# A DiT block: q and k by feature through VectorE's 32x32 transposes and DRAM instead of TensorE's transposes

## The chip, the cores and the metric

The kernel runs on one core of one Trainium2 chip, in one launch, in float32. A core has TensorE (PE, with the weight loads shown apart as PEld), VectorE (DVE), ScalarE (ACT), GpSimd (POOL) and SyncE (SP). SP, ACT and POOL also issue DMAs; in the profile the queue of SP is SPq. The metric is the device time of the launch in microseconds (us), the median of the runs; smaller is better.

## The reference

The input x is [2, 2048, 576]: batch 2, 2048 tokens, 576 features; 16 heads of 36 features; the hidden layer of the MLP has 2304. The condition c gives six rows of 576 by one product (shift, scale and gate for the attention part and for the MLP).

```python
mod = silu(c) @ w_ada + b_ada          # sh_msa, sc_msa, g_msa, sh_mlp, sc_mlp, g_mlp
xn  = ln(x, 1e-6) * (1 + sc_msa) + sh_msa
qkv = (xn @ w_qkv + b_qkv).reshape(B, N, 3, 16, 36)
q   = ln(q, 1e-5, qn_g, qn_b)          # over the 36 features of a head
k   = ln(k, 1e-5, kn_g, kn_b)
attn = softmax(einsum('bqhd,bkhd->bhqk', q, k) * 36 ** -0.5)
o   = einsum('bhqk,bkhd->bqhd', attn, v).reshape(B, N, 576) @ w_proj + b_proj
x   = x + g_msa * o
xn2 = ln(x, 1e-6) * (1 + sc_mlp) + sh_mlp
x   = x + g_mlp * (gelu(xn2 @ w1 + b1) @ w2 + b2)
```

The gain and bias of the head norms (qn_g, qn_b, kn_g, kn_b) have one value for each of the 36 features of a head. They are what the change calls scale and bias.

## The kernel before

`block_of_small` is the path that runs with these inputs. For each of the two batches it has three stages, and after both the MLP follows (two products with 7 instead of 8 sub-products each, at 2184 to 3176 us).

**Inputs** (`inputs`, about 62 to 251 us in the first batch, 1110 to 1329 in the second). A loop over the 16 token tiles of 128 tokens. In each turn TensorE makes three products, q, k and v (`product`: two halves of 288 columns, four matmuls on whole chunks and two on the last one each); VectorE adds the bias as it takes them out of PSUM (`biased`); `centred` subtracts each head's mean; ScalarE squares the result into `sq`; `head_scale` of the tile before takes the variance, ScalarE its root, VectorE the reciprocal, and GpSimd multiplies (`both` times `inv`). `by_feature(t - 2, ...)` then turns the finished q and k rows of the tile two back into columns: nine TensorE transposes of 128x128 into PSUM (line 993), and nine evictions, each applying gain and bias per partition: c < 4 by ScalarE (line 998), the other five by VectorE (line 1002). The result lies in SBUF, features on partitions: chunks 0 to 4 in `qo`, 5 to 8 in `kr`. Beside it runs the preparation of the rows two tiles on: the load of x, its norm on VectorE, a 32x32 transpose of all blocks on VectorE (`squares_turned`, line 898), four DMAs from GpSimd's queue that put the squares in their transposed places in a DRAM tensor `turned` (line 903), and DMAs that read it back by feature (`xnt`), which ScalarE modulates.

**Attention** (`attend`, about 251 to 1032 us and 1329 to 2104). 128 steps over (pair of heads, block of 512 queries, group g of keys). In each step TensorE makes `scores` (8 key-by-query banks: 32 features of a head in `km`, `qm`, the other 4 split into a high and a low part in `ke`, `qe`), ScalarE takes the exponential of 8 banks, and TensorE makes `values` of the step before. `take_q`, `take_k` and `take_k_block` issue the DMAs that bring the rows of a pair of heads into `qm`, `qe`, `km`, `ke` (`rows_taken`), and return a function (`parted`: two VectorE operations per 512 columns) that is called later. In the inputs they are started by `by_feature` itself: after tile 3 the first q block and key tiles 0 to 3, after tiles 7, 11, 13 and 15 the key tiles up to there; the returned function is called in the next `by_feature`, before the next tile is turned over. The last two tiles are turned by the `hooks` of the first steps of attention: nine transposes each, in two parts, at steps (0,0,0), (0,0,1), (0,1,0) and (0,1,1).

**Outputs** (`outputs`): the projection, its gate and the residual, and in the first batch the preparation of the second's inputs. Unused parts of `kr` serve as row buffers (`spare`).

The order on TensorE and VectorE is that of the program (`manual_schedule`), in attention also that of GpSimd and ScalarE; the order on the DMA queue of SP, and on ScalarE and GpSimd in the inputs, is set by a scheduler. Each queue runs its instructions in order: an instruction that waits holds up all behind it. In the inputs PSUM is four tiles of two banks (`s_tile`), each taken by one product, or by half of the transposes of a tile; in attention eight single banks.

Of the kernel before, what the change touches and what calls it, by code (L numbers as in the profile page):

```python
# [31 lines left out]
def dit_block(  # L32
# [230 lines left out]
    gb_qk = const.tile([P, 2, NQK], F32, name="gb_qk")  # L263
    gain_qk, bias_qk = gb_qk[:, 0, :], gb_qk[:, 1, :]
# [23 lines left out]
    with psum_pools(), tc.tile_pool(name="ada", bufs=2) as ada:  # L288
        raw = ada.tile([P, NKC, B], F32, name="raw")
        nc.sync.dma_start(out=raw[:, 0:FULL, :], in_=cond_t[0:512, :].rearrange("(p k) b -> p k b", k=FULL))  # L290
        for r0 in (0, 64):
            nc.sync.dma_start(out=raw[r0 : r0 + 64, FULL, :], in_=cond_t[512:576, :])
        nc.sync.dma_start(out=x_first[:, :C], in_=x[0, 0:P, :])
        was = ada_weights(ada, (1, 0))
        nc.gpsimd.memset(sil, 0.0)
        nc.scalar.activation(sil[:, :, 0:B], raw, AF.Silu)
        first_biases = feature_biases(ada, (1, 0), nc.gpsimd)
        rows_dram = dram.tile([2, 2, H, HD], F32, name="rows_dram")
        gb_rows = ada.tile([2 * NQK, P], F32, name="gb_rows")
        for i, ins in enumerate(((qn_g, kn_g), (qn_b, kn_b))):  # L300
            for w in range(2):
                nc.gpsimd.dma_start(out=rows_dram[i, w], in_=ins[w].partition_broadcast(H))
        nc.gpsimd.dma_start(
            out=gb_rows, in_=rows_dram.rearrange("i w h d -> (i w h d)").rearrange("(c p) -> c p", p=P)
        )
        rows_normed(ada, x_first)

        turned = s_tile()
        for k in range(NKC):
            nc.tensor.transpose(  # L310
                turned[:, k // FULL, k % FULL * P : (k % FULL + 1) * P], x_first[:, k * P : (k + 1) * P], ident
            )
        nc.scalar.copy(x_first[:, :512], turned[:, 0, :])
        nc.scalar.copy(x_first[:, 512:], turned[:, 1, :P])
        features(feature_rows(ada, was, first_biases), (1, 0))
        gb_ps = s_tile()[:, 0, : 2 * NQK]
        nc.tensor.transpose(gb_ps, gb_rows, ident[: 2 * NQK, : 2 * NQK])
        nc.vector.tensor_copy(gb_qk.rearrange("p i c -> p (i c)"), gb_ps)
# [440 lines left out]
    def block_of_small():  # L759
# [25 lines left out]
        high = kv.tile([P, BLK], F32R, name="high")  # L785
        met = kv.tile([1, 1], F32, name="met")
# [16 lines left out]
        def chunk(c, cols):  # L803
            return qo[:, c, cols] if c < NKC else kr[:, c - NKC, cols]


        def rows_taken(queue, main, ends, halves, first, src, dst):

            for c in halves:
                for h in range(2):  # L810
                    r0 = 32 * (2 * c + h)
                    for i, row, d, n in head_rows(first + h * HD, DIMS):
                        queue.dma_start(out=main[r0 + d : r0 + d + n, dst], in_=chunk(i, src(c))[row : row + n, :])
                    ((i, row, _, n),) = head_rows(first + h * HD + DIMS, HD - DIMS)
                    values = chunk(i, src(c))[row : row + n, :]
                    queue.dma_start(
                        out=ends[r0 : r0 + 4 * n, dst],
                        in_=values.unsqueeze(1).to_broadcast([n, 4, values.shape[1]]),
                    )

        def parted(ends, rows, low, sign):

            n = min(ends.shape[1], BLK)
            for c0 in range(0, ends.shape[1], n):
                part, up = ends[rows, c0 : c0 + n], high[rows, :n]
                nc.vector.tensor_scalar(up, part, sign[rows, :], None, ALU.mult)
                nc.vector.scalar_tensor_tensor(
                    part.bitcast(F32R), part, low[rows, :], up.bitcast(F32), ALU.mult, ALU.add
                )

        def take_k(p):
            m, e = km[p % 2], ke[p % 2]
            if p > 2:
                not_sooner(m)
                not_sooner(e)
            src = lambda c: slice(c * N // 2, (c + 1) * N // 2)
            rows_taken(nc.gpsimd, m, e, range(2), C + p * 2 * HD, src, slice(0, N // 2))
            return lambda: parted(e, slice(0, P), low_k, sign_k)

        def take_k_block(t0, t1):  # L840

            c, k0 = divmod(t0 * P, N // 2)
            dst = slice(k0, k0 + (t1 - t0) * P)
            rows_taken(nc.sync, km[0], ke[0], (c,), C, lambda c: slice(t0 * P, t1 * P), dst)
            return lambda: parted(ke[0][:, dst], slice(64 * c, 64 * c + 64), low_k, sign_k)

        def take_q(p, qb):
            i = qb % 2
            src = lambda c: slice(qb * BLK, (qb + 1) * BLK)
            rows_taken(nc.sync, qm[i], qe[i], range(2), p * 2 * HD, src, slice(0, BLK))  # L850
            return lambda: parted(qe[i], slice(0, P), low_q, sign_q)
# [94 lines left out]
        def inputs(b, weights, work, xnt, rows, loaded):  # L946
# [5 lines left out]
            def banks_of_two():  # L952
                return [bank for ps in (s_tile(), s_tile()) for bank in (ps[:, 0], ps[:, 1])]

            def centred(both, w0=0, w1=2):
# [10 lines left out]
                if w0 == 0:  # L966
                    squares["sq"] = work.tile([P, 2 * C], F32, name="sq")
# [20 lines left out]
            def by_feature(t, banks, chunks=range(NQK), all_on_vector=False, per=4):  # L988
                both, begun = normed[t], [*taken]
                taken.clear()  # L990
                parts = [(c, banks[i // per][:, i % per * P : i % per * P + P]) for i, c in enumerate(chunks)]
                for c, ps in parts:
                    nc.tensor.transpose(ps, both[:, c * P : (c + 1) * P], ident)  # L993

                for c, ps in parts[::-1]:
                    dst = chunk(c, slice(t * P, (t + 1) * P))
                    if c < 4 and not all_on_vector:
                        nc.scalar.activation(
                            dst, ps, AF.Identity, bias=bias_qk[:, c : c + 1], scale=gain_qk[:, c : c + 1]
                        )  # L1000
                    else:
                        nc.vector.tensor_scalar(
                            dst, ps, gain_qk[:, c : c + 1], bias_qk[:, c : c + 1], ALU.mult, ALU.add
                        )
                for do in begun:
                    do()
                if t == TPB - 1:
                    taken.append(take_q(0, 0))
                if t + 1 in key_tiles and NQK - 1 in chunks:
                    i = key_tiles.index(t + 1)  # L1010
                    taken.append(take_k_block(*key_tiles[i - 1 : i + 1]))

            def last(t, chunks):


                per = 3 if b == 0 and len(chunks) > 4 else 4
                by_feature(t, [bank() for _ in range(0, len(chunks), per)], chunks, True, per)
                left = [*taken]
                taken.clear()
                return left  # L1020
# [33 lines left out]
            for t in range(NT - 2):  # L1054
# [20 lines left out]
                biased(2, v, t, both)  # L1075
                if t >= 2:
                    by_feature(t - 2, banks_of_two())
# [4 lines left out]
            for t in range(NT - 2, NT):  # L1082
# [3 lines left out]
                for w in range(3):  # L1086
# [5 lines left out]
                    if w == (1 if t % 2 == 0 else 0):  # L1092
                        if t + 1 < NT:
                            input_modulated(b, ahead)
                        by_feature(t - 2, banks_of_two())
# [7 lines left out]
                before, xnt = both, ahead  # L1103

# [4 lines left out]
        def attend(b, pool, hooks):  # L1109
# [64 lines left out]
            behind, later = None, [[] for _ in range(5)]  # L1174
            for p, qb, g in [*steps, (None, None, None)]:
                pts = None if p is None else scores(p, qb, g)
                if g == 0 and (p, qb) != (NPAIR - 1, NBLK - 1):
                    later[2].append(take_q(*((p, qb + 1) if qb + 1 < NBLK else (p + 1, 0))))
                if g == 1 and qb == 1 and p + 1 < NPAIR:
                    later[4].append(take_k(p + 1))  # L1180
# [28 lines left out]
        spare = [kr[:, c, a * 640 : a * 640 + C] for c in range(4) for a in range(3)]  # L1209
# [115 lines left out]
        for b in range(B):  # L1325
# [11 lines left out]
            def last_inputs_done():  # L1337
                last_inputs(NT - 1, range(NKC - 1))
                close_work()

# [17 lines left out]
            def output_opened():  # L1358
# [3 lines left out]
                (0, 0, 0): lambda: last_inputs(NT - 2, range(NKC - 1, NQK)),  # L1362
                (0, 0, 1): lambda: last_inputs(NT - 1, range(NKC - 1, NQK)),
                (0, 1, 0): lambda: last_inputs(NT - 2, range(NKC - 1)),
                (0, 1, 1): last_inputs_done,
# [35 lines left out]
            if b + 1 < B:  # L1401
# [5 lines left out]
                def turned_of(t):  # L1407
                    squares = spare[9 + t % 3]
                    return (lambda x1: first.append(squares_turned(x1, nc.gpsimd, squares))) if t <= TPB else None

                with tc.manual_schedule(engines={mybir.EngineType.DVE}):
                    outputs(b, wp, {12: [lambda: input_modulated(b + 1, xnt)]}, spare[:9], turned_of)
# [389 lines left out]
```

## Time and profile before

| | |
|---|---|
| median of 3 runs | 3178.82 us (3177.3 to 3179.14) |
| profiled execution, its own time | 3178.22 us |
| its span in the profile | 3176.4 us |
| TensorE busy in the span | 3152.3 us, 99% |
| VectorE, ScalarE, GpSimd busy | 48%, 48%, 21% |
| granted TensorE clock, mean | 0.999 |

The span is what the profiler saw; the own time of that execution is 1.8 us more and lies 0.6 us under the median. Busy is the time in which an engine had an instruction in work; overlapping matmuls count once. "Released by" or "<-" names what ended a wait.

### The profile page before, as it was taken

Reading aid. Unit: us, or ns where it says so; the run is one execution under the profiler, and the core shown is the slowest. Engines: PE = TensorE matmul, PEld = TensorE weight load, DVE = VectorE, ACT = ScalarE, POOL = GpSimd, SP = SyncE. Lnnn points to the kernel's source line nnn. Section 1 sums busy time; section 2 is a strip of 40 time slices with the busy share of each in tenths; the row PEclk is TensorE's granted clock in tenths of the full one; section 3 lists DMA queues with packets and bytes.
Section 4 is the critical chain, followed back from the end, with each engine's and each line's share of the span. In section 5 each row is a group of like instructions: output and inputs, shape, how many; then the busy total and the mean of one; then the engine's idle time right before and its main releaser. Section 6 shows DMA issues by size and latency. Waiting matters only on the chain.

```text
span 3176.4 us, 47350 instructions
## 1 busy us (share of the span) xinstructions
PE 3152.3 (99%) x17833; PEld 1892.8 (60%) x17833; DVE 1511.0 (48%) x2212; ACT 1515.4 (48%) x2953; POOL 670.3 (21%) x933
## 2 busy tenths in 40 slices
PE   8999999999999999999999999999999999999999
PEld 6884333333333788733333333358888888777777
DVE  5774333333333577633333333346566554445454
ACT  2335666666666034466666666643555552000000
POOL 4551000112110355400001111013333320212121
PEclk9999999999999999999999999999999999999999
DMA  5322212223221633211222223146544434333331
GB/s 150 77 66 69 74 34 69 65 71 80 66 75 41 196 69 73 61 53 44 50 46 65 69 64 72 51 154 206 159 136 137 133 109 154 118 124 112 119 105 39
DMA packets 154537, 290.04 MB, mean 91 GB/s; under 512 B 34419, under 2 KB 86844, under 8 KB 152188
## 3 DMA queue, kind: packets, MB, share of 16 engines
q1 hardware_dynamic: 106212, 170.47, 17.7%
q0 software_dynamic: 44544, 110.85, 14.0%
q10 hardware_dynamic: 3544, 5.60, 0.5%
q8 instruction: 143, 2.34, 0.3%
q14 instruction: 94, 0.77, 0.1%
HBM read 153.95 MB, written 84.63 MB: 75 GB/s over the span
## 4 chain that ended last, share of the span: by engine, by line
PE 98%; DVE 1%; DMA 1%; SPq 0%; ACT 0%; issue 0%; ACTq 0%; DVEq 0%
PE b L1140 29%; PE b L1127 19%; PE s L1714 15%; PE m L1555 12%; PE s L1033 11%; PE s L413 4%; PE m L1569 2%; PE one L1555 2%; PE s L1035 1%; PE s L993 1%; PE s L424 1%; DMA bq<-in_w_qkv_dram 0%; DMA wq<-in_w_qkv_dram 0%; PE b L192 0%; DVE var L973 0%; DMA km<-qo 0%
## 5 line engine op out<-in xcount | busy, mean ns | idle before, releaser
L1131 ACT ACTIVATE pt<-b 128x512 f32<-128x512 f32 x2048 | 1057.8, 608 | 486.3 <-PE b L1140 272.2
L1140 PE MATMUL b<-pt,vt 128*64 128x512 f32 x4096 | 935.0, 598 | 0.0
L1140 PEld LDWEIGHTS b<-pt,vt 128*64 128x64 f32 x4096 | 271.8, 136 | 582.0 <-issue 439.4
L1127 PE MATMUL b<-qm,km 32*128 32x512 f32 x4096 | 568.1, 614 | 0.9 <-DVE vt L1044 0.6
L1188 DVE TENSOR_TENSOR ot<-b,ot 128x512 f32<-128x512 f32 x192 | 132.8, 692 | 652.2 <-PE b L1140 651.7
L1127 PE MATMUL b<-qe,ke 16*128 16x512 f32 x2048 | 423.7, 790 | 0.0
L1033 PE MATMUL s<-wq,xnt 128*128 128x288 f32 x1536 | 406.6, 408 | 3.6 <-DMA wq<-in_w_qkv_dram 2.8
L1127 PEld LDWEIGHTS b<-qm,km 32*128 32x128 f32 x4096 | 192.3, 184 | 270.5 <-ACT pt L1131 208.4
L1714 PE MATMUL s<-ws,as 128*128 128x288 f32 x1440 | 351.8, 406 | 0.0
L1033 PEld LDWEIGHTS s<-wq,xnt 128*128 128x128 f32 x1536 | 281.7, 191 | 65.8 <-DVE rstd L278 3.0
L1714 PEld LDWEIGHTS s<-ws,as 128*128 128x128 f32 x1440 | 273.6, 190 | 75.6
L1159 DVE RECIPROCAL den<-den 128x512 f32<-128x512 f32 x64 | 213.6, 3337 | 9.3 <-DMA den<-den_dram 9.3
L1555 PE MATMUL m<-xnt,wb 128*128 128x256 f32 x864 | 210.2, 379 | 0.9 <-issue 0.9
L1555 PE MATMUL m<-s,wb 128*128 128x256 f32 x864 | 210.0, 379 | 0.0
L1186 DVE COPY ot<-b 128x512 f32<-128x512 f32 x64 | 44.3, 692 | 334.0 <-PE b L1140 334.0
L903 POOL DMA_DIRECT2D turned<-squares x220 | 148.3, 680 | 258.7 <-DVE squares L898 235.3
L1555 PEld LDWEIGHTS m<-s,wb 128*128 128x128 f32 x864 | 164.2, 190 | 22.3
L1127 PEld LDWEIGHTS b<-qe,ke 16*128 16x128 f32 x2048 | 108.3, 184 | 114.4 <-issue 113.1
L1555 PEld LDWEIGHTS m<-xnt,wb 128*128 128x128 f32 x864 | 158.9, 190 | 20.3 <-issue 1.3
L1244 POOL DMA_DIRECT2D kr<-in_x_dram x32 | 17.6, 549 | 726.9 <-DVE met L790 726.9
L1593 ACT ACTIVATE cs<-cs,b_sb 128x512 f32<-128x512 f32 x144 | 98.8, 719 | 115.1 <-DVE cs L1588 93.1
L1714 PE MATMUL s<-ws,hidden 128*128 128x288 f32 x576 | 142.3, 406 | 0.0
(199 smaller groups left out, 3012.0 us busy)
## 6 DMA issues: line engine op xcount, KB each, us to landing
gelu<-cs SPq DMA_DIRECT2D x144, 256.0 KB
hidden<-gelu SPq DMA_DIRECT2D x16, 2304.0 KB
den<-den_dram SPq DMA_DIRECT2D x128, 128.0 KB
turned<-squares POOLq DMA_DIRECT2D x220, 72.0 KB, 2.5
xnt<-turned POOLq DMA_DIRECT2D x56, 256.0 KB, 3.8
x_dram<-kr POOLq DMA_DIRECT2D x48, 288.0 KB, 3.4
qm<-qo SPq DMA_DIRECT2D x192, 64.0 KB
kr<-in_x_dram POOLq DMA_DIRECT2D x34, 288.0 KB, 3.8
```

The source lines that it names most:

```text
L413: nc.tensor.matmul(outs[a], stationary(k, a), moving(k, a), start=(first and k == 0), stop=(not first and k == FULL - 1),)
L903: queue.dma_start(out=by_square[g], in_=squares[g * SQ : (g + 1) * SQ, :].rearrange("p (k j) -> p k j", j=SQ))
L1033: nc.tensor.matmul(out_a, full[:, k, :], wq[:, k, f], start=k == 0, stop=False)
L1127: nc.tensor.matmul(ps, k[r, keys], q[r, :], start=first, stop=not first)
L1131: nc.scalar.activation(pt[:, h, :], banks[2 * c + h], AF.Exp, scale=SCALE)
L1140: nc.tensor.matmul(acc[64 * h : 64 * h + 64, :], vt[:, v0 : v0 + 64], pt[:, h, :], start=pt is pts[0][0], stop=pt is pts[-1][0],)
L1159: nc.vector.reciprocal(den, den)
L1188: nc.vector.tensor_tensor(ot, acc, ot, ALU.add)
L1555: nc.tensor.matmul(out_m[m], wb[:, slot[m], k, f * P : (f + 1) * P], moving[m](k), start=k == 0 and m in (1, 2, 5, 6), stop=k == 1 and m == 1,
L1569: nc.tensor.matmul(out_m[m], wr[w][:, f * P : (f + 1) * P], a[:, i, t * PAIR : (t + 1) * PAIR], start=False, stop=i == 1 and m != 2,)
L1593: nc.scalar.activation(part, part, AF.Gelu, bias=b1_sb[:, g : g + 1])
L1714: nc.tensor.matmul(ms[m], stationary[m][:, f, :], ws[m][:, f, :], start=(f == 0), stop=(f == HF - 1))
```

## The change

`by_feature` no longer uses TensorE and PSUM. VectorE transposes all 32x32 blocks of the tile's q and k rows at once (128x1152) into one of three parts of `kr`, and four DMAs on SP's queue write them into a DRAM tensor `qk` of [1152, 2048], features by tokens, in runs of 32 values. `rows_taken` reads its rows from there, so one DMA serves the 32 features where one or two stood before. Gain and bias are applied in attention to the rows taken: `scaled` on `qm` and `km`, and inside `parted` on `qe` and `ke`, with the values by row from `gb_at`, which two small matmuls with a selection make once (`gains_by_row`, after tile 1 of the first batch). The buffer `sq` moves into `kr`. The last two tiles are turned over at the end of the inputs and in the first step of attention, not in four steps of it. `spare` has 11 buffers and `outputs` of the first batch uses 8 row buffers instead of 9.

```diff
-        gb_rows = ada.tile([2 * NQK, P], F32, name="gb_rows")
+        nc.gpsimd.memset(gb_rows, 0.0)
...
-                nc.gpsimd.dma_start(out=rows_dram[i, w], in_=ins[w].partition_broadcast(H))
+                nc.gpsimd.dma_start(out=gb_rows[:HD, i, w : w + 1], in_=ins[w].unsqueeze(1))
...
-        nc.tensor.transpose(gb_ps, gb_rows, ident[: 2 * NQK, : 2 * NQK])
-        nc.vector.tensor_copy(gb_qk.rearrange("p i c -> p (i c)"), gb_ps)
...
         def rows_taken(queue, main, ends, halves, first, src, dst):
-                    for i, row, d, n in head_rows(first + h * HD, DIMS):
-                        queue.dma_start(out=main[r0 + d : r0 + d + n, dst], in_=chunk(i, src(c))[row : row + n, :])
+                    queue.dma_start(out=main[r0 : r0 + DIMS, dst], in_=qk_rows["dram"][f0 : f0 + DIMS, src(c)])
...
+        def gains_by_row():
+            at = {i: kr[:, i, 2 * C : 2 * C + P] for i in range(2)}
...
+            nc.vector.tensor_copy(
+                at[0][0:DIMS, :].rearrange("p (i d) -> p i d", d=DIMS),
+                ident[0:DIMS, 0:DIMS].unsqueeze(1).to_broadcast([DIMS, 4, DIMS]),
+            )
+            for i in range(4):
+                nc.vector.tensor_copy(
+                    at[1][DIMS : 2 * DIMS, 32 * i : 32 * i + 16].rearrange("p (d r) -> p d r", r=4),
+                    ident[DIMS : 2 * DIMS, DIMS:HD].unsqueeze(2).to_broadcast([DIMS, 4, 4]),
+                )
+            ps = s_tile()[:, 0, 0:8]
+            for i, sel in at.items():
+                nc.tensor.matmul(
+                    ps[:, 4 * i : 4 * i + 4], sel, gb_rows.rearrange("p i w -> p (i w)"), start=True, stop=True
+                )
+            nc.vector.tensor_copy(gb_at.rearrange("p e i w -> p (e i w)"), ps)
+
+        def scaled(dst, part, rows, w, of_ends=0):
+            gain, bias = (gb_at[rows, of_ends, i, w : w + 1] for i in range(2))
+            nc.vector.tensor_scalar(dst, part, gain, bias, ALU.mult, ALU.add)
 
-        def parted(ends, rows, low, sign):
+        def parted(ends, rows, w):
...
-                nc.vector.tensor_scalar(up, part, sign[rows, :], None, ALU.mult)
+                scaled(value, part, rows, w, 1)
+                nc.vector.tensor_scalar(up, value, sign[rows, :], None, ALU.mult)
...
         def take_k_block(t0, t1):
...
-            return lambda: parted(ke[0][:, dst], slice(64 * c, 64 * c + 64), low_k, sign_k)
+            def made():
+                scaled(km[0][rows, dst], km[0][rows, dst], rows, 1)
+                parted(ke[0][:, dst], rows, 1)
+            return made
...
         def take_q(p, qb):
-            return lambda: parted(qe[i], slice(0, P), low_q, sign_q)
+            return [lambda: scaled(qm[i], qm[i], full, 0), lambda: parted(qe[i], full, 0)]
...
-            def by_feature(t, banks, chunks=range(NQK), all_on_vector=False, per=4):
-                for c, ps in parts:
-                    nc.tensor.transpose(ps, both[:, c * P : (c + 1) * P], ident)
-                for c, ps in parts[::-1]:
...
+            qk_rows["dram"] = dram.tile([2 * C, N], F32, name=f"qk{b}")
+            by_square = qk_rows["dram"].rearrange("(k d) (t g j) -> t g d k j", d=SQ, g=P // SQ, j=SQ)
+            def by_feature(t):
+                squares = kr[:, t % 3, 0 : 2 * C]
+                nc.vector.transpose(squares, normed[t])
+                for g in range(P // SQ):
+                    nc.sync.dma_start(
+                        out=by_square[t, g], in_=squares[g * SQ : (g + 1) * SQ, :].rearrange("p (k j) -> p k j", j=SQ)
+                    )
                 for do in begun:
                     do()
...
+                if b == 0 and t == 1:
+                    gains_by_row()
                 if t >= 2:
-                    by_feature(t - 2, banks_of_two())
+                    by_feature(t - 2)
...
+            by_feature(NT - 2)
...
-                    later[2].append(take_q(*((p, qb + 1) if qb + 1 < NBLK else (p + 1, 0))))
+                    for i, do in enumerate(take_q(*((p, qb + 1) if qb + 1 < NBLK else (p + 1, 0)))):
+                        later[1 + i].append(do)
...
-                (0, 0, 0): lambda: last_inputs(NT - 2, range(NKC - 1, NQK)),
-                (0, 0, 1): lambda: last_inputs(NT - 1, range(NKC - 1, NQK)),
-                (0, 1, 0): lambda: last_inputs(NT - 2, range(NKC - 1)),
-                (0, 1, 1): last_inputs_done,
+                (0, 0, 0): last_inputs_done,
```

## The prediction

> **What bounds the kernel now.** I read the page's busy times and its chain first, then TensorE's timeline in the inputs and at the opening of attention, then busy time and DMA share by stretch, then the groups that the change touches.
>
> ```profile
> PE 3152.3 (99%) x17833; PEld 1892.8 (60%) x17833; DVE 1511.0 (48%) x2212; ACT 1515.4 (48%) x2953; POOL 670.3 (21%) x933
> ...
> PE 98%; DVE 1%; DMA 1%; SPq 0%; ACT 0%; issue 0%; ACTq 0%; DVEq 0%
> ```
>
> TensorE runs without a gap and the chain lies on it, so what leaves its queue shortens the kernel unless a wait takes its place. How long the nine transposes of a tile hold the queue is read from starts, not from durations that overlap:
>
> ```profile
> 80.09 1.15 PE L993 MATMUL s<-ident,both 128*128 128x128 f32 x9
> 81.08 2.11 PE L1033 MATMUL s<-wq,xnt 128*128 128x288 f32 x8
> ...
> 94.30 1.15 PE L993 MATMUL s<-ident,both 128*128 128x128 f32 x9
> 95.28 2.11 PE L1033 MATMUL s<-wq,xnt 128*128 128x288 f32 x8
> ```
>
> They take 0.98 us of a tile's 14.21; the products are 13.22. What stands beside it in such a tile and over the inputs (columns: span, then PE, PEld, DVE, ACT, POOL busy, clock, DMA share, GB/s):
>
> ```profile
> 80.09:94.30 14.21, 14.21 (x72) 11.69 (x71) 10.84 (x19) 5.59 (x13) 8.79 (x11) 1.00 0.35 76
> ...
> 62.00:250.00 188.00, 188.00 (x918) 154.79 (x917) 145.33 (x257) 72.38 (x167) 95.64 (x122) 1.00 0.29 66
> ```
>
> VectorE is busy 77% of the inputs, the DMA engines 29%, about 4 us of a tile. The groups:
>
> ```profile
> L993 PE MATMUL s<-ident,both 128*128 128x128 f32 x252 | 32.1, 272 | 0.0
> L1002 DVE TENSOR_SCALAR kr<-s,gb_qk 128x128 f32<-128x128 f32 x112 | 38.1, 402 | 5.8 <-PE s L993 5.8
> L898 DVE STREAM_TRANSPOSE squares<-xt 128x576 f32<-128x576 f32 x37 | 28.8, 779 | 1.3
> L826 DVE TENSOR_SCALAR high<-qe,part 128x512 fp32r<-128x512 f32 x64 | 30.6, 478 | 0.1
> L827 DVE SCALAR_TENSOR_TENSOR qe<-qe,part,high 128x512 fp32r<-128x512 f32 x64 | 48.1, 751 | 2.3
> ```
>
> **Removed.** 14 groups of nine in each batch's input loop: 28 x 0.98 = 27.4 us. The other two tiles of a batch are turned in attention (0.7 + 0.7 + 0.6 + 0.6 us); these I count with the opening below. ScalarE loses four evictions a tile, VectorE five; neither is on the path.
>
> **Moved to VectorE, in the inputs.** Five evictions (starts to end about 2.0 us) give way to one transpose of 128x1152: twice the 779 ns less the fixed part, 1.5 us. VectorE's tile, waits on ScalarE included, adds up to 11.5 us of 13.2: covered, with 1.7 us to spare; without that cover each us over costs 28 us. Here the Trainium skill ("VectorE: DVE Perf Modes", "Rules for kernel authors") speaks against the change: transpose 128x128 on TensorE if PSUM will do. Its table in "The three transpose paths" has 390 ns on TensorE and 311 on VectorE, 32x32 blocks only. The trace has 0.11 us a piece on TensorE and 1.5 us for all nine on VectorE. By the table (estimate, 9 x 0.311 = 2.8 us) VectorE would need 12.8 of 13.2 us; by the row, 11.5. The sum is the same, the margin not. The row decides.
>
> **The four DMAs a tile.** A nearest row is `turned`: 72 KB in the same runs of 128 B; in the window 78 to 82 us four of them filled 0.44 + 0.60 + 0.85 + 0.05 of the engines, 0.48 us each. At 144 KB: 0.97, four 3.9 us. With the 4 us of before, 8 of 13.2: no bound. SP's queue is nearly empty there.
>
> **Attention's own work.** Per query block (four steps of 5.98 us) VectorE gains two operations of about 0.5 us, per pair of heads about 2 us, on 5.33 us busy of 11.97. The DMAs of `take_q` run one block ahead (issued 324.5 for use at 352) and `scaled` is called after the block's first step, some 7 us after they land. Cost 0; without the cover a late q block would hold VectorE, the eviction of `values` behind it and then TensorE, 1 us for 1 us, at most 64 times.
>
> **gains_by_row.** TensorE's two matmuls stand behind v of tile 1 and wait for VectorE: its eviction (0.2 + 0.68), five small copies (0.2 each), then the matmuls. TensorE stands 2.2 us, once (1 to 3). The transpose of gb_rows that goes had ScalarE's wait beside it: 0.
>
> **The queue order, which the source does not show.** In the program built from the changed kernel SP's queue has the first of the four writes of tile 4 ahead of the twelve DMAs of `take_q` and `take_k_block` that follow tile 3; so too for tiles 8, 12 and 14. Such a write waits for VectorE's transpose of its tile. VectorE, right behind that transpose, runs `scaled` and `parted`, which wait for those very DMAs. Before, they were issued a tile sooner and VectorE did not wait. What one takes on SP:
>
> ```profile
> 116.17 0.52 SPq L813 DMA_DIRECT2D qm<-qo  x1
> 116.73 0.69 SPq L816 DMA_DIRECT2D qe<-qo  x1
> 117.47 0.51 SPq L813 DMA_DIRECT2D qm<-qo  x1
> 118.03 0.69 SPq L816 DMA_DIRECT2D qe<-qo  x1
> ```
>
> 0.65 to 0.7 us each. From S, the start of q of tile 7: transpose of tile 4 done at 2.5, its write issued at 3.1, eight q DMAs by 8.5, four of k by 11.3, landed 2 us later. VectorE is free again at about S + 15 instead of 7. Behind it: head means, q's eviction, norm and squares of tile 9 (S + 21.5 instead of 8.6); then four DMAs (2.7), GpSimd's multiply (2.1), the loads (landed 31), ScalarE's squares, root and modulation (31.4 to 34). TensorE needs tile 9 at S + 26.4 and ends its q near 36 instead of 30.8: 5 us lost. PSUM's four tiles cover the rest. Tile 8 has four DMAs only: VectorE loses 2.5 + 0.6 + 2.8 + 2 - 2.5 = 5.4 us, which the 4 to 5 us of slack before modulation nearly absorb: 0.3. Per batch 5.3, two batches 10.6; bounds 0 (the DMAs land sooner) and 16.
>
> **The opening of attention.** Let E be the end of the last v. Tile 12's wait (5.5 us) comes two tiles before E, so v's eviction, at 253.3 before (E + 1.6), comes at E + 8.6, the last root on ScalarE at E + 7.5, then its table load (1.3), then exponentials; the first `values` starts at E + 14 instead of E + 8.5.
>
> ```profile
> 260.01 3.65 PE L1140 MATMUL b<-pt,vt 128*64 128x512 f32 x16
> ...
> 267.47 3.65 PE L1140 MATMUL b<-pt,vt 128*64 128x512 f32 x16
> ...
> 274.70 3.65 PE L1140 MATMUL b<-pt,vt 128*64 128x512 f32 x16
> ```
>
> Then tile 15 goes through transpose (E + 11.6), SP (four k DMAs of tile 13, three writes, four of q, four writes: E + 20), landing (23), four DMAs (26), landing (28), `scaled` and `parted` (29); the fourth scores need it. The third `values` starts at E + 30.5 instead of E + 23.2; from there four transposes' worth, 1.3 us, is saved, and the shift left is about +5. In the second batch no weights stand between: +3.5. Sum 8.5 (bounds -6, if VectorE is in time and only the transposes go, and +16).
>
> **Sum.** -27.4 + 2.2 + 10.6 + 8.5 = -6.1 us: the profiled 3178.22 becomes 3172.1, the median, 0.6 above it, 3172.7.
>
> **Rivals.** (1) *The queue order costs nothing*: the taken rows land within VectorE's slack. For: DMAs of SP land within 2 us of their issue, and 1.7 us a tile are to spare. Against: VectorE's program has nothing between the transpose and the waiting operation. Then -27.4 + 2.2 + 0 to 2, about 3154.
>
> (2) *The 128-byte writes make the inputs bound by DMA*; slower. The Trainium skill ("DMA: Bandwidth & Descriptors", "Specifications") asks 512 B for line rate; below that the engine reads, modifies and writes. The row has this in it: 152 GB/s in those writes, 287 in the window of loads at 84 us. By the row four writes cost 3.9 us. If from SP they cost double (an estimate, as a rule of two transfers for one), 7.8, the engines are taken for 11.8 of 13.2 us, and `xnt`, which now lands some 5 us into a tile, lands near 11.5. Modulation takes 2.5, so past 10.7 every us is paid in each tile: 0.8 x 26 = 21 us more, 3194. The write of 144 KB decides it: above 1.6 us each. For: they fall together with the loads. Against: the measured rate.
>
> (3) *The waits of the queue order are worse*, each stall not absorbed: upper bounds, -27.4 + 3 + 16 + 16: +8, 3187.
>
> **How the numbers follow.** Main case 0.53, 3172.7, its own range 3164 to 3181; as its centre lies at the edge of what can be told from no change (0.2%, 6.4 us), 0.28 of it is faster, 0.22 the same, 0.03 slower. Rival 1: 0.22, faster. Rivals 2 and 3: 0.25, slower. Faster 0.50, same 0.22, slower 0.28. Range 3156 to 3188: it leaves out the end of rival 1 and most of rival 2.
>
> **What would show it.** Right: tiles of 13.2 us with no PE group at line 993; a wait of `qm` or `km` in `scaled` on DMA of 6 to 8 us after the transposes of tile 4 and of about 5 after tiles 8 and 12; an idle stretch of TensorE near tile 9; first `values` some 14 us after the last v. Wrong: no such waits (rival 1), tiles longer than 13.4 us all along or `xnt` waited for by ScalarE in each (rival 2), steps of attention longer than 5.98.

## The result: 1.3% slower

The changed kernel takes 3218.86 us, median of four runs (3217.19 to 3224.0), against 3178.98 of the kernel before beside it: ratio 1.0127, 95% interval 1.011 to 1.0145, 40 us more. The forecast was 3172.7 with a range of 3156 to 3188. The profiled execution took 3224.0 us (span 3222.2), 5.1 over the median; the sums below are made on this span against the 3176.4 of before, 45.8 us apart.

The busy times and the chain of the page after:

```profile
PE 3152.4 (98%) x17548; PEld 1876.1 (58%) x17548; DVE 1607.4 (50%) x2263; ACT 1475.5 (46%) x2841; POOL 660.7 (21%) x927
...
PE 87%; DVE 6%; DMA 3%; SPq 1%; issue 1%; ACT 0%; POOL 0%; DVEq 0%; POOLq 0%; ACTq 0%
```

TensorE is as busy as before with 285 matmuls fewer, and the chain is no longer its own: 98% fell to 87%. What took its place is in TensorE's waits (us in total, times, longest):

```profile
PE b L1150 <- DVE km L836: 11.0, 2, 7.9
PE s L306 <- DVE x_first L283: 10.3, 1, 10.3
PE s L1053 <- ACT xnt L949: 8.1, 3, 5.0
PE b L1150 <- DVE both L1061: 7.7, 2, 3.8
PE b L1150 <- DVE vt L1064: 5.4, 2, 3.1
PE s L1053 <- DVE squares L927: 5.2, 1, 5.2
PE b L1150 <- DVE ot L1213: 5.2, 8, 0.7
```

The second is the start of the kernel, there before as well; of the others none was above 0.9 us. By stage, from the first product of a stage on TensorE to that of the next (the last column is the best kernel of the experiments):

| us | before | after | three mends (e7) |
|---|---|---|---|
| inputs, first batch | 232.4 | 232.3 | 220.7 |
| attention, first batch | 780.5 | 800.8 | 781.7 |
| outputs, first batch | 71.6 | 72.8 | 71.6 |
| inputs, second batch | 225.4 | 221.3 | 212.0 |
| attention, second batch | 774.8 | 803.5 | 780.9 |

By the forecast the inputs were to lose 6.2 and 8.4 us (13.7 a batch for the transposes, less the waits and `gains_by_row`); they lost 0.1 and 4.1. Attention, which was to pay 8.5 in all, pays 20.3 and 28.7.

**An ordinary tile is what was forecast.** Busy time by stretch (columns: span, then PE, PEld, DVE, ACT, POOL busy, clock, DMA share, GB/s), for the tile that answers to the one of 14.21 us:

```profile
80.08:93.31 13.23, 13.23 (x63) 10.71 (x62) 10.31 (x16) 4.09 (x9) 7.57 (x11) 1.00 0.60 115
```

TensorE has no gap in it and nothing but products. VectorE does 10.3 us, and the DMA engines are taken for 0.60 x 13.23 = 7.9 us. VectorE's transpose of 128x1152 takes 1.36 us (mean of 32).

**The queue order.** VectorE's timeline behind the transpose of tile 4, then SP's in the same microseconds:

```profile
122.85 1.37 DVE L1022 STREAM_TRANSPOSE kr<-both 128x1152 f32<-128x1152 f32 x1
130.90 0.55 DVE L836 TENSOR_SCALAR qm<-qm,gb_at 128x512 f32<-128x512 f32 x1 [6.68 <-DMA qm<-qk]
```

```profile
124.24 0.30 SPq L1024 DMA_DIRECT2D qk<-kr  x1
124.78 0.80 SPq L805 DMA_DIRECT2D qm<-qk  x1
125.64 0.78 SPq L807 DMA_DIRECT2D qe<-qk  x1
...
131.53 0.62 SPq L807 DMA_DIRECT2D ke<-qk  x1
132.19 1.97 SPq L1024 DMA_DIRECT2D qk<-kr  x3
```

The transpose ends at 124.22, the first write of tile 4 goes out, and only behind it come the DMAs that VectorE's next operation waits for. The wait is 6.68 us here, 6.42 and 5.06 behind tiles 8 and 12; in the second batch 7.13, 5.41 and 3.94.

**What TensorE makes of it.** Its timeline at tile 9, and the stretches of the idle time, of the matmuls behind it, and the same for the later stall at tile 13:

```profile
147.95 0.64 PE L1055 MATMUL s<-wq,xnt 128*128 128x288 f32 x2
153.60 4.21 PE L1053 MATMUL s<-wq,xnt 128*128 128x288 f32 x8 [5.01 <-ACT xnt L949]
157.20 1.09 PE L1055 MATMUL s<-wq,xnt 128*128 128x288 f32 x2
158.09 2.25 PE L1053 MATMUL s<-wq,xnt 128*128 128x288 f32 x8
```

```profile
148.43:153.60 5.17, 0.16 (x2) 0.00 (x0) 4.67 (x10) 2.00 (x4) 1.29 (x3) 0.80 0.97 216
153.60:158.09 4.49, 4.49 (x11) 3.35 (x11) 3.97 (x6) 2.20 (x6) 3.89 (x6) 0.50 0.44 67
208.96:211.11 2.15, 0.16 (x3) 0.00 (x1) 1.68 (x5) 0.88 (x4) 0.00 (x0) 1.00 1.12 237
211.11:213.80 2.69, 2.57 (x10) 1.85 (x11) 2.17 (x4) 2.19 (x6) 2.11 (x4) 1.00 0.30 45
```

The stall is 5.0 us, as forecast; but the ten matmuls behind it take 4.49 us where they took 2.20, at a granted clock of 0.50. From 148.43, where the product was due, to 160.45, where the half after it starts, 7.6 us are lost (two halves take 4.4). The stall of 2.0 us at 209 leaves the clock at 1.00 and costs 2.6.

**The opening of attention**, first batch, from the chain of waits in order of time (start, us, what):

```profile
260.91 1.38 DVE kr L1022
262.30 0.30 SPq L1024
...
265.60 1.01 SPq L1024
...
273.68 3.54 DMA qk<-kr
...
278.40 2.58 DMA km<-qk
281.07 0.43 DVE km L836
281.50 0.09 issue
281.59 0.92 PE b L1150
```

The last v ended at 251.4 (the E of the prediction). From the transpose of tile 14 the path runs along SP's queue for 11 us, waits 3.5 us for the last write to land, 2.6 for the rows, and reaches TensorE at E + 30.2. TensorE waits three times in each opening, up to 7.9 us, and its clock follows (two stretches of the first batch, two of the second):

```profile
256.33:261.05 4.72, 1.57 (x9) 0.67 (x9) 4.11 (x8) 2.17 (x4) 0.59 (x1) 0.61 0.50 76
261.05:267.80 6.75, 6.75 (x35) 4.10 (x35) 2.60 (x2) 5.29 (x11) 3.69 (x5) 0.51 0.62 120
1374.60:1382.50 7.90, 0.04 (x2) 0.03 (x1) 0.51 (x2) 0.00 (x0) 1.21 (x3) 0.65 0.85 190
1382.50:1387.30 4.80, 4.79 (x20) 2.63 (x21) 3.91 (x8) 1.09 (x2) 0.00 (x0) 0.50 0.06 21
```

The sixth `values` starts 55.8 us after the last product, before 43.1: 12.7 us lost; in the second batch 60.7 against 43.8, 16.8 us.

**Later in attention** a loss appears that no step of the prediction had; it stood there only as a sign of being wrong. Steps of 5.98 us become 7.7, at one place in each pair of heads from the 59th step on: four steps in the first batch, six in the second, where in two of the four places the next step is as long. VectorE and GpSimd at the first place:

```profile
634.72 0.69 DVE L1213 TENSOR_TENSOR ot<-b,ot 128x512 f32<-128x512 f32 x1 [1.63 <-PE b L1163]
635.33 0.13 DVE L784 COPY met<-kr 1x1 f32<-1x1 f32 x1
635.39 0.53 DVE L836 TENSOR_SCALAR kr<-ke,gb_at 128x512 f32<-128x512 f32 x1
635.95 2.08 DVE L845 TENSOR_SCALAR high<-kr,part 128x512 fp32r<-128x512 f32 x1
638.07 0.75 DVE L846 SCALAR_TENSOR_TENSOR ke<-kr,part,high 128x512 fp32r<-128x512 f32 x1
638.74 3.35 DVE L1182 RECIPROCAL den<-den 128x512 f32<-128x512 f32 x1
642.12 0.69 DVE L1183 TENSOR_TENSOR ot<-ot,den 128x512 f32<-128x512 f32 x1
642.73 0.68 DVE L1213 TENSOR_TENSOR ot<-b,ot 128x512 f32<-128x512 f32 x1
```

```profile
636.32 1.42 POOL L1272 TENSOR_TENSOR kr<-kr 128x576 f32<-128x576 f32 x1
```

The third part that `take_k` now returns (three operations, 1.8 us) falls in the step that also has the reciprocal of `den`. That alone costs the first three pairs 0.1 us each (steps of 6.1). From the 59th step on GpSimd adds residual rows in the same microseconds, and the operation at line 845 takes 2.08 us instead of its median 0.49. The eviction at 642.73 comes too late for the next scores: TensorE waits 0.65 us for it and starts the next `values` 1.76 us late. The same 2.08 us stands at all eight places.

The two further long steps of the second batch have another cause. TensorE waits the same 0.64 us, and the 16 matmuls of `values` right behind take 5.35 us in place of 3.65, at half the clock:

```profile
1933.04 5.35 PE L1163 MATMUL b<-pt,vt 128*64 128x512 f32 x16
...
1933.30:1936.70 3.40, 3.40 (x10) 0.98 (x8) 0.00 (x0) 1.18 (x3) 0.00 (x0) 0.50 0.17 52
```

At the other six places the clock stays at 1.00.

### The profile page after: what moved, and what is told of

It reads as the page before. It is cut to its first block, busy times and chain, and to the rows that moved or that the text cites. A ratio compares the mean times of both kernels' runs of the same rounds, so it can differ in the third digit from the quotient of the medians.

```text
span 3222.2 us, 46882 instructions
## 1 busy us (share of the span) xinstructions
PE 3152.4 (98%) x17548; PEld 1876.1 (58%) x17548; DVE 1607.4 (50%) x2263; ACT 1475.5 (46%) x2841; POOL 660.7 (21%) x927
## 4 chain that ended last, share of the span: by engine, by line
PE 87%; DVE 6%; DMA 3%; SPq 1%; issue 1%; ACT 0%; POOL 0%; DVEq 0%; POOLq 0%; ACTq 0%
PE b L1163 27%; PE b L1150 18%; PE s L1737 15%; PE m L1578 12%; PE s L1053 7%; PE s L406 3%; PE m L1592 2%; PE one L1578 2%; PE s L1055 1%; DVE den L1182 1%; DMA km<-qk 1%; DVE high L845 1%; DVE both L989 1%; DVE kr L1022 1%; SPq L805 0%
## 5 line engine op out<-in xcount | busy, mean ns | idle before, releaser
L1150 PE MATMUL b<-qm,km 32*128 32x512 f32 x4096 | 586.7, 622 | 29.3 <-DVE km L836 11.0
L1150 PE MATMUL b<-qe,ke 16*128 16x512 f32 x2048 | 436.6, 797 | 0.0
L1150 PEld LDWEIGHTS b<-qm,km 32*128 32x128 f32 x4096 | 199.1, 187 | 311.2 <-ACT pt L1154 209.6
L1269 POOL DMA_DIRECT2D kr<-in_x_dram x32 | 17.5, 546 | 748.7 <-DVE met L784 748.7
L1578 PEld LDWEIGHTS m<-xnt,wb 128*128 128x128 f32 x864 | 158.9, 190 | 20.3 <-issue 1.3
```

The source lines that it names most:

```text
L1150: nc.tensor.matmul(ps, k[r, keys], q[r, :], start=first, stop=not first)
L1578: nc.tensor.matmul(out_m[m], wb[:, slot[m], k, f * P : (f + 1) * P], moving[m](k), start=k == 0 and m in (1, 2, 5, 6), stop=k == 1 and m == 1,
```

## The experiments

Each is the changed kernel with the edit shown. Times are medians; ratios are to the kernel before beside them, and the changed kernel's is 1.0127.

**e1: SP in the order of the program.**

```diff
-            with tc.manual_schedule(engines={mybir.EngineType.DVE}):
+            with tc.manual_schedule(engines={mybir.EngineType.DVE, mybir.EngineType.SP}):
                 last_inputs = inputs(...)
```

> SP's queue in the inputs in the order of the program: the DMAs that take q and k rows stand behind the writes of their own tile, not behind the first write of the next. Theory of the queue order: VectorE's waits in scaled near 124, in the inputs, fall from 6.7 us to under 1, TensorE's idle stretches of 5.0 and 2.0 us (first batch) and 5.2 and 1.1 us (second) go with the slow matmuls behind them, v of the last tile comes some 10 us sooner in the first batch and 8 in the second, and the opening of attention, which starts with less left for VectorE, gains about 5 in each: in all 25 us less than the changed kernel. Rival, the 128-byte writes are slow to land whatever the order: the waits stay within 1 us of what they were, and the time too.

Measured: 3193.23 us, 1.0039 (1.0025 to 1.0053), 25.6 less. The inputs fall to 223.9 and 212.2 us, the sixth `values` comes 4.1 and 4.3 us sooner after the last product. The waits for `qm` are 0.8 us; one for `km` of 2.4 stays in the inputs, and TensorE keeps two stalls of 0.7. So the order of SP's queue was the cause of the inputs' waits, and of 8.4 us of what the openings lost.

**e2: the rows scaled one tile later**, the queue left to the scheduler.

```diff
...
-                begun = [*taken]
+                begun = [*before_last]
+                before_last[:] = taken
                 taken.clear()
...
```

> The queue is left to the scheduler, but the functions that scale the taken rows are called one tile later. Theory of the queue order: VectorE has 13 us between the DMAs and the first operation that needs them, so the waits and TensorE's idle stretches of the inputs go as with the order of the program, 18 us over both batches; the opening may gain less, since the rows of tiles 12 and 13 are scaled behind the transpose of the last tile. Rival, that the transfers land late whatever VectorE does: a wait of some us remains at the later place.

Measured: 3198.58 us, 1.0058 (1.0042 to 1.0075), 20.3 less. The inputs now take 219.2 and 211.8 us, with no stall: 13.2 and 13.6 us under before. The second is all but the whole of the 13.7 that the transposes were to give a batch. The first has the 1.8 us of `gains_by_row` against it, and for it a first tile that ran 1.5 us shorter than before's, by its waits for the weights. In the opening VectorE's waits for `km` reach 12.9 us and the sixth `values` still comes at 53.0 and 58.9. So the inputs' part and the opening's part are two losses.

**e3: the second half of a k's ends one step later.**

```diff
...
-                        later[4 + i].append(do)
+                        later[(4, 5, 7)[i]].append(do)
```

> The second half of the ends of a k (three VectorE operations) moves from the step with the reciprocal of den to the step behind it. Both theories expect that the steps of 7.74 us (four in the first batch, six in the second) become 5.98 to 6.1: 17 us less than the changed kernel. If they stay, another operation makes them.

Measured: 3203.59 us, 1.0071 (1.0054 to 1.0088), 15.3 less; no step of 7.7 is left in either batch. From the sixth `values` to the last, attention takes 734.1 and 727.7 us; before it was 733.8 and 727.4, in the changed kernel 741.4 and 738.4.

**e4: the residual rows one step sooner**, VectorE's operations left where they are.

```diff
-                (3 + t // NBLK, t % NBLK, 3): lambda t=t: residual_begun(b, t) for t in range(NT + 1)
+                (3 + t // NBLK, t % NBLK, 2): lambda t=t: residual_begun(b, t) for t in range(NT + 1)
```

> The residual rows that GpSimd adds in attention are begun one step sooner, in no step with a reciprocal; VectorE's operations stay in their steps. Theory of the port: the operation of 2.08 us for 0.49 is one that GpSimd's addition of 1.42 us holds up, and without it the step has room: steps of 7.74 become about 6.1 and 14 us go, though some operation in the step before is held up in its place. Rival, VectorE simply has too much in that step (two operations on PSUM, a division and three of k): the steps stay at 7.7.

Measured: 3203.64 us, 1.0071, 15.2 less; again no step of 7.7. VectorE's and GpSimd's timelines one step ahead of the reciprocal, then the reciprocal's step:

```profile
628.07 2.08 DVE L845 TENSOR_SCALAR high<-kr,part 128x512 fp32r<-128x512 f32 x1
...
634.00 0.49 DVE L845 TENSOR_SCALAR high<-kr,part 128x512 fp32r<-128x512 f32 x1
...
635.20 3.35 DVE L1182 RECIPROCAL den<-den 128x512 f32<-128x512 f32 x1
```

```profile
628.44 1.41 POOL L1272 TENSOR_TENSOR kr<-kr 128x576 f32<-128x576 f32 x1
```

The 2.08 us went with GpSimd's addition to another instance of line 845, and the one beside the reciprocal is back at 0.49. So the hold-up belongs to the addition, not to the step; and it hurts only where the step has no room: VectorE's other work there is 0.69 + 0.53 + 0.49 + 0.75 + 3.35 + 0.69 + 0.68 = 7.2 us of 5.98, which it can just carry by being early, and not with 1.6 more. In e3 the addition (637.49 to 638.90) runs beside the reciprocal (636.56 to 639.89), which keeps its 3.33 us. The Trainium skill ("SBUF — State Buffer", "Who interferes with whom") has VectorE and GpSimd share a pair of SBUF ports under an exclusive lock that a tensor_scalar in a two-port mode takes and for which the loser waits out the other's whole instruction. The rows agree in size: 2.08 is about 0.49 and the addition's 1.42 together. They do not show the mode of the operation. The page also gives the ports to whoever issues first, and by the recorded starts that was VectorE, by 0.37 us (635.95 against 636.32). So that the hold-up comes with the addition is shown; that it is this lock is argued.

**e5: e2 and e4 together.**

> The functions that scale the taken rows called one tile later, and the residual rows of attention begun one step sooner, together. If the two causes are separate their gains add, 20 and 15 us: 35 less than the changed kernel, near the kernel before (3180 to 3186). If they share a cause, less than 25.

Measured: 3182.69 us, 1.0008 (0.9999 to 1.0016), 36.2 less. The two causes add.

**e6: the opening alone.** Tile 14 is turned over inside the last tile's products, the rows of the last two key tiles are taken on GpSimd's queue, and the first hook runs before the next block of q is asked for.

```diff
+                    if t == NT - 1 and w == 1:
+                        by_feature(NT - 2)
...
-            by_feature(NT - 2)
...
+            queue = nc.gpsimd if t1 == NT else nc.sync
...
+                if (p, qb, g) == (0, 0, 0):
+                    later[1] = hooks.pop((0, 0, 0))() + later[1]
                 if g == 0 and (p, qb) != (NPAIR - 1, NBLK - 1):
```

> The changed kernel with another order at the opening of attention alone: tile 14 is turned over 6 us sooner on VectorE, the rows of the last two key tiles are taken from GpSimd's queue, and the next block of q is asked for after the writes of the last tile. Theory of the chain at the opening (the transpose of the last tile, eight DMAs of q ahead of its four writes, two loads of weights ahead of its rows, then scaled): VectorE's wait for km in front of the third scores falls from 9 to 14 us to under 4, and 10 to 16 us go over both batches. Rival, the opening is late because VectorE still has the stall of tile 12 behind it: the wait for km only changes place, and less than 5 us go.

Measured: 3219.91 us, 1.0127 (1.0111 to 1.0142): nothing gained, against what the theory said. VectorE's timeline:

```profile
253.79 1.37 DVE L1023 STREAM_TRANSPOSE kr<-both 128x1152 f32<-128x1152 f32 x1
260.54 0.42 DVE L836 TENSOR_SCALAR km<-km,gb_at 64x256 f32<-64x256 f32 x1 [5.38 <-DMA km<-qk]
...
266.47 0.70 DVE L1065 TENSOR_TENSOR vt<-s,bq 128x576 f32<-128x576 f32 x1
```

With `by_feature(14)` sooner, the scaling of tiles 12 and 13, called in it, is sooner too, and now waits 5.4 us ahead of the norms of the last tile and the eviction of its v. TensorE waits 14.5 us for that v in place of the later wait for `km`. The wait changed its place, as the rival said; its reason was the scaling called right behind a transpose, the same as in the inputs. e6 holds three edits at once, and no run tells apart what each does.

**e7: e2, e4 and e6 together.**

> All three together: scaled rows called one tile later, residual rows sooner, the other order at the opening. If the removed transposes are worth their 27 us in the inputs and the opening's loss of 12 and 17 us is the chain of its DMAs, the time is 3165 to 3172, 8 to 15 us under the kernel before. If the opening keeps a loss that no order mends (VectorE has three transposes and two norms to do behind the last product), it stays at 3178 to 3184.

Measured: 3160.81 us (3159.39 to 3165.35), ratio to the kernel before 0.9943 (0.9929 to 0.9956): 18 us faster than it, and below what was expected. Its chain:

```profile
PE 98%; DMA 1%; DVE 0%; SPq 0%; issue 0%; ACT 0%; ACTq 0%; DVEq 0%
```

With the rows scaled one tile later, the order of e6 is worth 22 us (3182.69 to 3160.81); without it nothing. VectorE's waits for `km` are 6.5 us in two places, the sixth `values` comes at 43.3 and 48.0 us. Left over are about 4 us in the second opening.

**e8: every write of q and k made twice**, on top of e7.

> The kernel with three mends, and every 32x32-block write of q and k done a second time, into a DRAM tensor that nobody reads: four more DMAs of 144 KB a tile on SP's queue, behind the four that count. The tiles of the three mends take 13.22 us with the DMA engines taken for 0.58 of it. Theory: the writes have room, at 0.2 to 0.25 of a tile for four of them; twice as many fill 0.8, the tiles stay at 13.2 us and the time within 5 us of the three mends (the opening, where the writes of the last tile stand ahead of rows that are waited for, may lose 3). Rival, the 128-byte writes bound the inputs as soon as the loads fall together with them: tiles of 14 us and more, 20 us in all.

Measured: 3222.2 us, 1.0125 (1.011 to 1.0141), 61 over e7. Two stretches of its inputs, before the first rows are taken and behind, and the matmuls behind two of TensorE's waits (2.07 and 2.75 us):

```profile
62.00:120.00 58.00, 58.00 (x265) 46.90 (x264) 45.06 (x68) 16.97 (x39) 31.03 (x41) 1.00 0.74 135
...
180.00:200.00 20.00, 17.93 (x78) 14.17 (x77) 10.36 (x15) 6.73 (x16) 7.86 (x11) 0.95 0.70 131
...
197.79:201.70 3.91, 3.91 (x10) 2.81 (x11) 0.73 (x2) 3.12 (x7) 0.45 (x1) 0.56 0.88 137
...
230.62:233.00 2.38, 2.33 (x9) 1.62 (x9) 1.29 (x2) 2.08 (x6) 1.29 (x4) 1.00 0.89 124
```

Up to 150 us TensorE has no gap, with the DMA engines taken for 0.74 of the first stretch. From there on, with the rows being taken as well, it stalls five times in the first batch (1.0 to 2.8 us): the inputs take 238.2 and 223.9 us, and the openings lose 12 and 23 us against e7. `xnt` lands 5.2 us after its issue, 4.0 in e7, and SP spends 4.1 + 4.3 us and more of a tile on issuing. Whether SP's queue or the engines make the most of the 61 us, this run does not tell apart. It shows that four writes a tile fit and that eight do not: the margin was smaller than I had it.

**e9: e7 and e3.**

> The three mends, and the second half of the ends of a k moved out of the step with the reciprocal as well. If the residual rows were all that overfilled that step, nothing is left to gain: within 2 us of the three mends (six steps of 6.1 for 5.98 become 5.98: 0.7 us a batch). If VectorE was still late there, up to 4 us less.

Measured: 3162.25 us, 0.994 (0.9926 to 0.9954): no different from e7. The trace has the expected gain all the same: the steps of 6.1 of each `take_k` are gone, and attention from the sixth `values` to the last is 0.8 us shorter a batch than in e7, less than the runs differ.

## Why the prediction was wrong

| term, us over both batches | forecast | after |
|---|---|---|
| transposes gone from the inputs | -27.4 | -27.4 |
| gains_by_row | +2.2 | +1.8 |
| waits of the queue order in the inputs | +10.6 | +19.6 |
| opening of attention | +8.5 | +29.5 |
| attention behind its opening | 0 | +19.5 |
| outputs | 0 | +1.2 |

They sum to 44.2 of the 45.8; 1.4 more is a longer first tile, with its waits for the weights. Tile 1 takes 15.0 us where those behind it take 13.2: that is `gains_by_row`, 1.0 of it TensorE's wait. Of the 19.5 behind the opening 17.5 are the ten long steps, 14.1 in the eight that VectorE makes and 3.4 in the two at half the clock.

*Removed and moved.* Right: tiles of 13.23 us, VectorE's transpose 1.36 us for 1.5, DMA 7.9 us of a tile for 8. e2 gives the inputs back nearly whole. So the rule that rather TensorE should transpose 128x128 did not decide here: the row did. (The times of the table that the prediction cites are for one bf16 tile; these rows are float32.)

*The four DMAs a tile.* Right as a sum, at four writes; "no bound" held with less room than thought, as e8 shows.

*The queue order.* The mechanism was right, in its place and in VectorE's waits (6.68 for 6 to 8; 6.42 and 5.06 for about 5), and so was the first stall of TensorE, 5.0 us at tile 9. Two sizes were off. "5 us lost" left out the clock: matmuls at 0.50 behind the stall made it 7.6 us (7.7 in the second batch). The Trainium skill states it ("TensorE: Matmul & The Clock Gate", "Part 1: The HAM clock gate"): the clock halves after an idle window of about 3.4 us. By it the 5.0 us stall is billed twice and the 2.0 us stall not, as the rows of these two have it; the sum had only the first bill. Other rows do not keep to such a length: the clock fell to 0.50 behind two waits of 0.64 us in attention and, in e8, to 0.56 and 0.59 behind 2.07 and 2.30 us, and stayed at 1.00 behind 2.75. So the runs decide against a fixed length, and what does set it below 5 us stays open. And tile 8's wait, put at 0.3 because slack "nearly absorbs" it, cost 2.6 and 1.7 us.

*The opening of attention.* This step was mis-sized most: 5 and 3.5 forecast, 12.7 and 16.8 measured. v's eviction came when forecast (E + 9.0 for 8.6). In the second batch this was luck: tile 12's wait was 3.9 us there and not 5.5, and a subtraction of VectorE beside a GpSimd multiply of 2.13 us took 3.27 for 0.76, which made up for it (E + 8.9). The first `values` came at E + 16.4 for 14, since TensorE, idle in pieces before, ran at 0.51 for 6.75 us. Then the path of the last rows was too short in the sum. A write took SP 1.0 us here (three in 3.00, four in 4.14), not 0.65 to 0.7, which was the price of DMAs with long rows; the last write landed after 3.5 us, not 2. And at E + 29 the rows were to be ready in time for a delay of 7 us in the third `values`, 5 net: it came at E + 35.7, 12.6 late, and the scores behind the rows ran at a clock of 0.50 too, for 5.5 us. In the second batch "no weights stand between" was wrong: SP issued a load of `wp` (1152 KB) right ahead of the last rows, which were issued by 1375.4 and landed at 1382 in a stretch where the DMA engines were taken for 0.85 of the time. That this load made them late was not tried.

*Attention's own work.* "Cost 0" was the step that failed. The count of VectorE's work was a mean over two steps, 5.33 us of 11.97, and did not ask in which step each part lands: one part of `take_k` lands beside the reciprocal of 3.3 us, and beside GpSimd's addition from the fourth pair on. That took 19.5 us. I had priced what happens without the cover, 1 us for 1 us, and had not checked the cover step by step. e3 and e4 each take the 15 us back.

*Rivals.* Rival 1 would hold for the inputs alone with the order mended (e1, e2). Rival 3, worse waits, is what happened in kind, at +40 rather than +8. Rival 2 did not happen at four writes.

## What to carry to other kernels

Where an in-order engine consumes what a DMA brings, look in the built program at what stands ahead of that DMA in its queue, and put at least one whole tile between asking and using: one tile later was worth 20 us here, and made another reordering worth 22 that alone was worth nothing. Count an engine's cover by step, not as a mean, and with the other engine whose instructions can hold it up. A stall of TensorE can be paid again in slow matmuls behind it: both stalls of 5 us were, and of the shorter ones some.

## What the hardware showed that was not expected

- Behind 5.0 us of idle time TensorE ran 4.5 us at a granted clock of 0.50; behind 2.0 us it kept 1.00. But behind waits of 0.64 us in attention it ran 3.4 us at 0.50 twice in eight times.
- A VectorE tensor_scalar of 0.49 us took 2.08 beside a GpSimd addition of 1.42; the reciprocal beside the same addition kept its 3.33.
- SP took 0.30 to 3.04 us to issue a write of 144 KB in runs of 128 B, 0.85 in the mean. In a group of four the medians rise: 0.30, 0.58, 0.87, 1.25.
